# Turning a chunk's rows on VectorE and by small transfers in place of TensorE, in a block of a gated scan and a mixture of experts

## The chip, the cores and the metric

The kernel runs on one NeuronCore of a Trainium2 chip, in one launch. The metric is the device time in microseconds (us) of that core. The engines of a core work side by side, each through a queue of its own in program order: TensorE (PE, matrix products; its weight loads are PEld), VectorE (DVE), ScalarE (ACT), GpSimd (POOL) and SyncE (SP), which here only issues transfers. Engines wait for one another through semaphores. SBUF is the working memory of 128 partitions, PSUM the memory that TensorE writes to.

## The reference

`x` is [4, 1024, 256] in float32: 4 batches of 1024 tokens. The block is a modulated norm, a gated scan, a second modulated norm, and a mixture of 8 experts with the best two for each token:

```
mod = (silu(c) @ wmod).reshape(4, 6, 1, 256)      # sa, ca, ga, sb, cb, gb
h = layernorm(x) * (1 + ca) + sa

# the scan part
norm = sqrt(sum(h*h)) * D**-0.5
xn = rms_scale * h / (norm + 1e-8) * split_scale
K = sigmoid(xn @ W_K)                              # 256 -> 512
u, g_in, g_out = split(xn @ W_ugg, 3)              # 256 -> 3 x 512
u = u * sigmoid(g_in) * (1 - K)
s[t] = K[t-1] * s[t-1] + u[t]                      # along the tokens of a batch
x = x + ga * ((s * sigmoid(g_out)) @ W_out + h)

# the experts
h = layernorm(x) * (1 + cb) + sb
p = softmax(h @ Wg + bg); the best two, normed to 1
x = x + gb * sum over the two of p_e * (gelu(h @ W1[e] + b1[e]) @ W2[e] + b2[e])
```

## The kernel before

Tokens go through the first part in 8 chunks of 512 (two to a batch). A chunk lies in SBUF as [128 partitions, 4 groups, 256 channels]: token 128 n + p of the chunk is in partition p, group n. The products of the first part contract over channels, so the normed rows have to be turned: channels on partitions, tokens along the row, as `hT` [128, 2 halves of the channels, 512 tokens].

The order of the instructions on every engine is the order of the program text; nothing is reordered. One pass of the chunk loop (`c_`, from line 949) works on several chunks at once: the four quarters of the projections of chunk `c_` (`project`, quarters 0 to 3 of the 512 hidden channels), the preparation of the next chunk `nxt`, the output product and the second norm of the one before (`prv`), and the gate of the one before that (`old`). In a pass, TensorE does in order:

- `project(c_, 0)`: four products `pk`, `pgi`, `pu`, `pgo`, each of four matmuls with a moving operand of 128 x 512 taken from `hT`;
- `o_pe(prv)`: the output product `pya`, 32 matmuls;
- `f_turn(old)`: eight 128x128 turns of the second-norm rows `h2` into the PSUM tiles `ptf`, which ScalarE copies to `hT2` (L392);
- `project(c_, 1)`; then, in some passes, `r_rank_pe` (three small products, `pr`); then `f_gate(old)`: the router's 16 small products `pl`, with `hT2` as the stationary operand;
- `project(c_, 2)`; `project(c_, 3)`, in whose middle (between `pgi` and `pu`) stands `a_turn(nxt)`: eight turns of the scaled rows `u` of the next chunk into `pta`, which ScalarE scales by `rs_sb` and writes to `hT` (L390).

VectorE's work in a pass, around the change: in every quarter it takes `nu` (L431, which empties the PSUM tile of `pu`; L434), the scan (L440) and `z` (L441); ahead of quarter 2 `a_scale(nxt)` (L373 to L376) divides the rows `h` of the next chunk by their root mean square into `u`; ahead of quarter 3 `f_mod(prv)` (L484, L485) modulates the second-norm rows `h2`. The routing of a batch is spread over passes 3 to 7 and past the end: `r_softmax`, `r_first`, `r_second`, `r_place`; `r_second` ends with `chose`, `earlier` and `ended` (to L613), which `r_rank_pe` reads.

PSUM: `ps_mm` has four buffers, which `pk`, `pgi`, `pu`, `pgo` take in turn. The tile `u` has one buffer (tag "u"); `hT` has two, `hT2` one.

SP's queue issues every load and store of this part in program order: the load of `x` for chunk `c_ + 3` (L124), the store of `x` (`out_dram`, L467), the rows of the modulation (`mda`, `mdf`, `gb`, L312, L317, L325), `store_gb` (L329), the store of the second-norm rows `hx` (L495), and near the end the weights of the first blocks of experts (`fetch`, L804 to L807).

After the loop the work goes over into blocks of 256 tokens of one expert (`b_turn`, `b_up` with `ph`, `b_down` with `pye`), which gather rows of `hx` by lists that the routing wrote. The first two blocks are interleaved with what is left of the last chunk: `f_turn(last - 1)`, `r_second`, `b_up(0)`, `r_rank_pe`, `b_turn(1)`, `o_pe(last)`, `f_gate(last - 1)`, `f_mod_alone(last)`, `b_down(0)`, `f_turn(last)`, `b_up(1)`, `b_turn(2)`, `f_gate(last)`. The routing keeps a table `token` (L173) of the token number of each partition and group, which goes into the lists.

Chunk 0 is turned ahead of the loop, by TensorE, with code of its own (from L938).

Of the kernel before, what the change touches and what calls it, by code (L numbers as in the profile page):

```python
# [9 lines left out]
F32 = mybir.dt.float32  # L10
I32 = mybir.dt.int32
AF = mybir.ActivationFunctionType
# [7 lines left out]
def tile_adaln_block(  # L20
# [45 lines left out]
    TPB = TB // P  # L66
    TK = 256
    HK = TK // P
    LN_EPS = 1e-5
    RMS_EPS = 1e-8  # L70
    TOPK_EPS = 1e-8
# [92 lines left out]
    for e in range(E):  # L164
# [5 lines left out]
    nc.gpsimd.memset(again[:, :, 0:1], 0.0)  # L170
    count = const.tile([P, E], F32, tag="count", name="count")
    nc.gpsimd.memset(count, 0.0)
    token = const.tile([P, NT], F32, tag="token", name="token")  # L173
    nc.gpsimd.iota(
        token, [[P, NT]], base=0, channel_multiplier=1, allow_small_or_imprecise_dtypes=True
    )
    number = const.tile([P, NJ], F32, tag="number", name="number")
    nc.gpsimd.iota(
        number, [[1, NJ]], base=0, channel_multiplier=0, allow_small_or_imprecise_dtypes=True
# [191 lines left out]
    def a_scale(c_):  # L371
        h, ss, u = X[c_]["h"], X[c_]["ss"], X[c_]["u"]
        nc.vector.tensor_scalar_add(ss, ss, RMS_EPS)  # L373
        nc.vector.reciprocal(ss, ss)
        for n in range(TPB):
            nc.vector.tensor_scalar_mul(u[:, n, :], h[:, n, :], ss[:, n : n + 1])  # L376

    def a_skip(c_):

# [1 line left out]
        nc.vector.tensor_mul(h, h, wide_row(MDF[c_ // NB][:, 0, :]))  # L381
        nc.vector.tensor_add(xb, xb, h)

    def transposes(src, dst, what, scales):
        for k in range(KC):
            pt = ps_tr.tile([P, TB], F32, tag="tr", name=f"pt{what}_{k}")
            for t in range(TPB):
                nc.tensor.transpose(pt[:, ts(t, P)], src[:, t, ts(k, P)], ident)  # L388
            if scales:
                nc.scalar.activation(dst[:, k, :], pt, AF.Copy, scale=rs_sb[:, k : k + 1])  # L390
            else:
                nc.scalar.copy(dst[:, k, :], pt)  # L392

    def a_turn(c_):
        hT = deep.tile([P, KC, TB], F32, tag="hT", name=f"hT_{c_}")
        X[c_]["hT"] = hT
        transposes(X[c_]["u"], hT, f"a{c_}", True)

    def project(c_, hc, mid=()):


        hT = X[c_]["hT"]
        part = c_ % NB
        X[c_].setdefault("z", [])
        z = work.tile([P, TB], F32, tag="z", name=f"z_{c_}_{hc}", bufs=5)
        X[c_]["z"].append(z)
        kt = kts[part][hc]
        nu = work.tile([P, TB], F32, tag="nu", name=f"nu_{c_}_{hc}", bufs=2)
        go = work.tile([P, TB], F32, tag="go", name=f"go_{c_}_{hc}", bufs=2)

        def product(w, col, what):
            ps = ps_mm.tile([P, TB], F32, tag="mm", name=f"p{what}_{c_}_{hc}")
            for k in range(KC):
                nc.tensor.matmul(  # L414
                    ps,
                    lhsT=w[:, k, col : col + P],
                    rhs=hT[:, k, :],
                    start=(k == 0),
                    stop=(k == KC - 1),
                )  # L420
            return ps

        ps = product(wk_sb, hc * P, "k")
        nc.scalar.activation(kt[:, 1:], ps, AF.Sigmoid)
        if part < NB - 1:

            nc.scalar.activation(kts[part + 1][hc][:, 0:1], ps[:, TB - 1 :], AF.Sigmoid)
        nc.scalar.activation(nu, product(wu_sb, H + hc * P, "gi"), AF.Sigmoid)
        for step in mid:
            step()  # L430
        nc.vector.tensor_mul(nu, nu, product(wu_sb, hc * P, "u"))  # L431
        nc.scalar.activation(go, product(wu_sb, 2 * H + hc * P, "go"), AF.Sigmoid)

        nc.vector.scalar_tensor_tensor(nu, kt[:, 1:], 1.0, nu, ALU.subtract, ALU.mult)  # L434
        if part < NB - 1:
            s_ = ends[hc]
        else:
            s_ = work.tile([P, TB], F32, tag="s", name=f"s_{c_}_{hc}", bufs=2)
        first = 0.0 if part == 0 else ends[hc][:, TB - 1 :]
        nc.vector.tensor_tensor_scan(s_, kt[:, :TB], nu, first, ALU.mult, ALU.subtract)  # L440
        nc.vector.tensor_mul(z, s_, go)  # L441
# [56 lines left out]
            )  # L498
        )

    def f_turn(c_):
        hT = deep.tile([P, KC, TB], F32, tag="hT2", name=f"hT2_{c_}", bufs=1)
        X[c_]["hT2"] = hT
        transposes(X[c_]["h2"], hT, f"f{c_}", False)


    sh = [P, NT, E]
# [9 lines left out]
    def f_gate(c_):  # L517
        b, i = divmod(c_, NB)
        if i == 0:
            R[b] = {"p": small.tile(sh, F32, tag="p", name=f"p_{b}")}  # L520
        hT = X[c_]["hT2"]
        pl = ps_tr.tile([P, TPB, E], F32, tag="tr", name=f"pl_{c_}")
        for n in range(TPB):
            for k in range(KC):
                nc.tensor.matmul(  # L525
                    pl[:, n, :],
                    lhsT=hT[:, k, ts(n, P)],
                    rhs=wg_sb[:, k, :],
                    start=(k == 0),
                    stop=(k == KC - 1),  # L530
                )
        nc.vector.tensor_add(
            R[b]["p"][:, ts(i, TPB), :], pl, bg_sb.unsqueeze(1).broadcast_to((P, TPB, E))
        )
# [400 lines left out]
        all_rows(i)  # L935
    keep_busy(18)
    a_scale(0)
    hT = deep.tile([P, KC, TB], F32, tag="hT", name="hT_0")  # L938
    X[0]["hT"] = hT
    pts = [ps_tr.tile([P, TB], F32, tag="tr", name=f"pta0_{k}") for k in range(KC)]  # L940
    for t in range(TPB):
        for k in range(KC):
            nc.tensor.transpose(pts[k][:, ts(t, P)], X[0]["u"][:, t, ts(k, P)], ident)
    nc.scalar.activation(hT[:, 0, :], pts[0], AF.Copy, scale=rs_sb[:, 0:1])  # L944
    nc.vector.tensor_scalar_mul(hT[:, 1, :], pts[1], rs_sb[:, 1:2])
    other_rows()
    load_mdf(0)
    a_stats(1)
    for c_ in range(NCH):
        nxt, prv, old = c_ + 1, c_ - 1, c_ - 2  # L950
        more, was, been = nxt < NCH, prv >= 0, old >= 0
        b, part = divmod(c_, NB)

        route = old // NB if been and old % NB == NB - 1 else None
        placed = (c_ - 3) // NB if c_ >= 3 and (c_ - 3) % NB == NB - 1 else None


        if c_ + 3 < NCH:
            load_x(c_ + 3, nc.sync)
        if more:  # L960
            shift(nxt)
        project(c_, 0, [lambda: a_norm(nxt)] if more else [])
        drain(6)
        if more:
            a_mod(nxt)
        if was:
            a_skip(c_)
            o_pe(prv)
            o_resid(prv)
        if placed is not None:  # L970
            r_second(placed)
        if been:
            f_turn(old)
        if part == NB - 1:
            load_mdf(b + 1)


        if part == 0 and was:
            scale_out(b)
        if was:  # L980
            f_stats(prv)
        project(c_, 1, [lambda: a_square(nxt)] if more else [])
        if c_ == 0:
            first_contents()
        drain(6)
        if placed is not None:
            r_rank_pe(placed)
        if been:
            f_gate(old)
        if not more:  # L990
            fetch_weights(0)
            for j in range(NE):
                fetch_entries(j)

            wait_for(BK[0]["ld"], scattered)
            fetch_rows(0)
            fetch_rows(1)
        if part == 0:
            if c_ == 0:
                setup_ctx.close()  # L1000
                pools["w"] = ctx.enter_context(tc.tile_pool(name="weights", bufs=2))
            load_gb(b)
            load_mda(b + 1)
        elif c_ == 1:
            clear_rows()
            if c_ == 0:
                load_mdf(1)


        if more:  # L1010
            a_root(nxt)
        if was:
            shift(prv)
        if placed is not None:
            r_place(placed)
        if route is not None:
            r_softmax(route)
        if more:
            a_scale(nxt)
        project(  # L1020
            c_, 2,
            ([lambda: f_norm(prv)] if was else [])
            + ([lambda: r_exp(route)] if route is not None else []),
        )
        drain(6)
        if part == 0:
            store_gb(b)
        if c_ + 2 < NCH:
            a_stats(c_ + 2)


        if not was:
            a_skip(c_)
            scale_out(b)
        if was:
            f_mod(prv)
            f_store(prv)
        project(c_, 3, [lambda: a_turn(nxt) if more else b_turn(0)])
        drain(6)
        if route is not None:  # L1040
            r_first(route)
        if placed == EARLY_B - 1:
            tab["e"] = early_table()
# [1 line left out]

    last = NCH - 1
    fetch(0)
    f_turn(last - 1)
    r_second(B - 2)
    b_up(0)  # L1050
    r_rank_pe(B - 2)
# [6 lines left out]
    drain(4)  # L1058
    f_mod_alone(last)
    f_store(last)  # L1060
    b_down(0)
    f_turn(last)
    fetch(1)
    drain(6)
    b_up(1)
# [97 lines left out]
```

## Time and profile before

| | us |
|---|---|
| median of 3 runs (lowest, highest) | 818.54 (818.2, 821.06) |
| the profiled execution | 816.91 |
| its span, first to last instruction | 815.1 |
| first chunk's first product to last chunk's last product | 17.3 to 309.8 |
| eight turns `pta` or `ptf` on TensorE, from the first to the start of the next product | 0.87 |
| four matmuls of `pk` | 1.72 |
| ScalarE, two scalings of `hT` from `pta` | 1.26 |
| VectorE, four scalings of `u` | 1.14 |
| SP, one issue of a 512 KB store | 0.36 to 0.39 |
| landing of such a store, from its issue (median) | 3.3 to 3.7 |

The profiler records one execution: every instruction of every engine with its start and length. A row of the timeline merges neighbouring instructions of one line; matmul records overlap a little, since matmuls are pipelined, so the distance between the starts of two rows tells how long the first held TensorE. What ended a wait stands in brackets behind the idle time. The busy share of an engine is an average over stages that differ much.

### The profile page before, as it was taken

What the parts mean: (1) busy time and instruction counts of PE and PEld (TensorE: products, weight loads), DVE (VectorE), ACT (ScalarE), POOL (GpSimd) and SP (SyncE); (2) the same over time, 40 slices, a digit from 0 to 9 for tenths busy, and PEclk for the clock granted to TensorE, in tenths of its full rate; (3) what the DMA queues carried; (4) which work ended last, traced back from release to release, by engine and by line L of the source; (5) the groups of instructions that cost most, each with busy time, mean ns of one, the idle gap of its engine ahead of it and who ended that gap; (6) DMA issues with size and microseconds to landing.
All of it is one profiled execution on the core that took longest, in us unless ns stands there. A gap on an engine that the chain in (4) does not pass through costs nothing.

```text
span 815.1 us, 10691 instructions
## 1 busy us (share of the span) xinstructions
PE 800.9 (98%) x3479; PEld 608.3 (75%) x3479; DVE 350.1 (43%) x814; ACT 249.9 (31%) x574; POOL 299.1 (37%) x374
## 2 busy tenths in 40 slices
PE   8999999999999999999999999999999999999995
PEld 4464656464655558888888888888888888888984
DVE  5787776797688846554211211121121112112211
ACT  4434433535353243222222131222213122222231
POOL 2003010118203731788743433424343342434341
PEclk9999999999999999999999999999999999999998
DMA  8311231130102165598788687777777786776693
GB/s 286 118 42 56 86 101 49 52 98 26 46 26 85 27 181 170 146 255 200 197 238 242 177 237 202 218 197 221 203 210 232 204 226 196 212 196 191 195 292 81
DMA packets 107732, 130.76 MB, mean 160 GB/s; under 512 B 24647, under 2 KB 91787, under 8 KB 107665
## 3 DMA queue, kind: packets, MB, share of 16 engines
q1 hardware_dynamic: 88640, 104.11, 41.8%
q0 software_dynamic: 17456, 25.25, 13.9%
q10 hardware_dynamic: 1568, 0.57, 0.3%
q8 instruction: 34, 0.56, 0.3%
q14 instruction: 34, 0.27, 0.1%
HBM read 110.64 MB, written 21.75 MB: 162 GB/s over the span
## 4 chain that ended last, share of the span: by engine, by line
PE 94%; DMA 4%; DVE 1%; issue 0%; POOLq 0%; ACT 0%; SPq 0%; POOL 0%; DVEq 0%
PE ph_False L857 26%; PE pye_False L887 25%; PE pk L414 7%; PE pya L451 7%; PE pu L414 7%; PE pgo L414 7%; PE pgi L414 7%; DMA hb<-hx,ent 2%; PE ptx L841 2%; PE pl L525 2%; PE ptf L388 1%; PE pta L388 1%; DMA w<-in_L_ffn_W_dram 1%; PE idle L254 1%; PE pm L281 1%; DMA ent<-lists 1%
## 5 line engine op out<-in xcount | busy, mean ns | idle before, releaser
L887 PE MATMUL pye_False<-w,g_False 128*128 128x256 f32 x992 | 219.4, 379 | 0.0
L857 PE MATMUL ph_False<-xT,w 128*128 128x256 f32 x992 | 219.2, 379 | 0.0
L857 PEld LDWEIGHTS ph_False<-xT,w 128*128 128x128 f32 x992 | 188.3, 190 | 25.5
L887 PEld LDWEIGHTS pye_False<-w,g_False 128*128 128x128 f32 x992 | 186.1, 190 | 24.0
L866 ACT ACTIVATE g_False<-ph_False,bb 128x256 f32<-128x256 f32 x248 | 104.3, 473 | 312.8 <-issue 208.1
L874 POOL DMA_INDIRECT out_dram<-yb_False,ent x46 | 73.8, 1604 | 188.6 <-DVE yb_False L902 188.6
L843 DVE COPY xT<-ptx 128x512 f32<-128x512 f32 x37 | 25.6, 691 | 197.0 <-PE ptx L841 197.0
L901 DVE TENSOR_TENSOR yb_False<-pye_False,b2b 128x256 f32<-128x256 f32 x62 | 26.3, 425 | 154.7 <-PE pye_False L887 154.7
L544 POOL DMA_INDIRECT lists<-pay,placei x64 | 68.2, 1066 | 12.5 <-issue 11.5
L786 POOL DMA_INDIRECT hb<-hx,ent x56 | 59.0, 1054 | 18.7 <-issue 15.9
L414 PE MATMUL pk<-hT,wk_sb 128*128 128x512 f32 x128 | 60.9, 598 | 0.7 <-ACT hT L944 0.7
L414 PE MATMUL pu<-hT,wu_sb 128*128 128x512 f32 x128 | 60.2, 592 | 0.0
L414 PE MATMUL pgo<-hT,wu_sb 128*128 128x512 f32 x128 | 60.1, 592 | 0.0
L414 PE MATMUL pgi<-hT,wu_sb 128*128 128x512 f32 x128 | 60.1, 592 | 0.0
L214 POOL TENSOR_TENSOR rstd_f<-rstd_f,expo 128x4 f32<-128x4 f32 x8 | 8.2, 1019 | 132.5 <-DVE rstd_f L213 132.5
L451 PE MATMUL pya<-wo,z 128*128 128x256 f32 x256 | 56.6, 379 | 0.0
L451 PEld LDWEIGHTS pya<-wo,z 128*128 128x128 f32 x256 | 48.6, 190 | 9.5 <-issue 3.3
L414 PEld LDWEIGHTS pgi<-hT,wu_sb 128*128 128x128 f32 x128 | 24.3, 190 | 30.6 <-issue 30.4
L414 PEld LDWEIGHTS pgo<-hT,wu_sb 128*128 128x128 f32 x128 | 24.3, 190 | 30.6 <-issue 26.5
L414 PEld LDWEIGHTS pu<-hT,wu_sb 128*128 128x128 f32 x128 | 23.7, 190 | 26.8 <-issue 24.2
L414 PEld LDWEIGHTS pk<-hT,wk_sb 128*128 128x128 f32 x128 | 23.2, 190 | 24.5 <-issue 21.8
L431 DVE TENSOR_TENSOR nu<-nu,pu 128x512 f32<-128x512 f32 x32 | 22.0, 687 | 44.7 <-PE pu L414 33.0
(191 smaller groups left out, 760.9 us busy)
## 6 DMA issues: line engine op xcount, KB each, us to landing
w<-in_L_ffn_W_dram SPq DMA_DIRECT2D x72, 1024.0 KB, 6.5
b2b<-in_L_ffn_b_dram SPq DMA_DIRECT2D x36, 128.0 KB, 6.8
hx<-gb SPq DMA_DIRECT2D x4, 1024.0 KB, 4.8
out_dram<-x SPq DMA_DIRECT2D x8, 512.0 KB, 3.3
hx<-h SPq DMA_DIRECT2D x8, 512.0 KB, 3.7
x<-in_L_attn_x_dram SPq DMA_DIRECT2D x7, 512.0 KB, 5.3
wu_sb<-in_L_attn_W_ugg_dram SPq DMA_DIRECT2D x3, 512.0 KB, 5.5
mdf<-rows SPq DMA_DIRECT2D x4, 384.0 KB, 4.6
```

Of the source, the lines that this page charges most:

```text
L388: nc.tensor.transpose(pt[:, ts(t, P)], src[:, t, ts(k, P)], ident)
L414: nc.tensor.matmul(ps, lhsT=w[:, k, col : col + P], rhs=hT[:, k, :], start=(k == 0), stop=(k == KC - 1),)
L431: nc.vector.tensor_mul(nu, nu, product(wu_sb, hc * P, "u"))
L451: nc.tensor.matmul(py[:, t, :], lhsT=z[hc][:, ts(2 * q + t, P)], rhs=wo[:, hc, :], start=(hc == 0), stop=(hc == HC - 1),)
L544: ins = nc.gpsimd.indirect_dma_start(out=lists[:, :], out_offset=IndirectOffsetOnAxis(ap=place, axis=0), in_=what, in_offset=None, bounds_ ...
L786: nc.gpsimd.indirect_dma_start(out=g, out_offset=None, in_=hx[: seen(j), :], in_offset=IndirectOffsetOnAxis(ap=BK[j]["ent"][:, t, 0:1], ax ...
L843: nc.vector.tensor_copy(xT, pt)
L857: nc.tensor.matmul(ph[:, u, :], lhsT=w1[:, k, ts(fc, P)], rhs=xT[:, k, :n], start=(k == 0), stop=(k == KC - 1),)
L866: nc.scalar.activation(g[:, fc, :n], ph[:, u, :], AF.Gelu_apprx_tanh, bias=bb[:, fc : fc + 1])
L874: return nc.gpsimd.indirect_dma_start(out=out_rows[:n], out_offset=IndirectOffsetOnAxis(ap=at, axis=0), in_=yb, in_offset=None, bounds_che ...
L887: nc.tensor.matmul(py, lhsT=g[:, fc, ts(t, P)], rhs=w2[:, fc, :], start=(fc == 0), stop=(fc == FC - 1),)
L901: nc.vector.tensor_add(yb, py, b2b)
```

## The change

Only chunk 0 is still turned by TensorE. For chunks 1 to 7 `a_scale` writes the scaled rows in another order along the row (by quarter of the channels), `a_swap` then turns each 32 x 32 square in place with one VectorE instruction, and sixteen transfers on SP's queue, one for each pair of a source and a target quarter of the partitions, move 32 partitions x 1 KB each to their place in `hT`. `a_turn`, where it stood, only scales `hT` in place on ScalarE. `f_swap` does the same for the second-norm rows, with the reordering in the VectorE instruction, into a second tile of the tag "u" and by sixteen transfers into `hT2`; it stands after `f_store` ahead of quarter 3, one pass earlier than `f_turn` did for the same chunk. `hT` is now laid out [128, quarter of the source partitions, half of the channels, group, 32], so the moving operand of `project` is read in runs of 32 elements, and the router's logits come out with the tokens of a chunk in another order over partitions and groups, for which the table `token` is made anew by four instructions.

```diff
     token = const.tile([P, NT], F32, tag="token", name="token")
-    nc.gpsimd.iota(
-        token, [[P, NT]], base=0, channel_multiplier=1, allow_small_or_imprecise_dtypes=True
-    )
+    for n in range(TPB):
+        nc.gpsimd.iota(
+            token[ts(n, SQ), :].rearrange("p (c i) -> p c i", c=NB), [[TB, NB], [SQ, NQ]],
+            base=n * P, channel_multiplier=1, allow_small_or_imprecise_dtypes=True,
+        )
...
+        to = u.rearrange("p n d -> p (n d)").rearrange(
+            "p (q k n c) -> p n k q c", q=NQ, n=TPB, k=KC
+        )
         for n in range(TPB):
-            nc.vector.tensor_scalar_mul(u[:, n, :], h[:, n, :], ss[:, n : n + 1])
+            nc.vector.tensor_scalar_mul(
+                to[:, n], h[:, n, :].rearrange("p (k q c) -> p k q c", k=KC, q=NQ),
+                ss[:, n : n + 1],
+            )
...
-    def transposes(src, dst, what, scales):
+    turned = [P, NQ, KC, TPB, SQ]
+
+    def by_channel(hT):
+        return hT.rearrange("p i k n t -> p k n i t")
+
+    def swap(u, hT):
+        flat = u.rearrange("p n d -> p (n d)")
+        for q in range(NQ):
+            for i in range(NQ):
+                nc.sync.dma_start(
+                    out=hT[ts(q, SQ), i].rearrange("p k n t -> p (k n t)"),
+                    in_=flat[ts(i, SQ), ts(q, TPB * D // NQ)],
+                )
+
+    def a_swap(c_):
+        u = X[c_]["u"]
+        flat = u.rearrange("p n d -> p (n d)")
+        nc.vector.transpose(flat, flat)
+        X[c_]["hT"] = deep.tile(turned, F32, tag="hT", name=f"hT_{c_}")
+        swap(u, X[c_]["hT"])
+
+    def a_turn(c_):
+        hT = by_channel(X[c_]["hT"])
         for k in range(KC):
-            pt = ps_tr.tile([P, TB], F32, tag="tr", name=f"pt{what}_{k}")
-            for t in range(TPB):
-                nc.tensor.transpose(pt[:, ts(t, P)], src[:, t, ts(k, P)], ident)
-            if scales:
-                nc.scalar.activation(dst[:, k, :], pt, AF.Copy, scale=rs_sb[:, k : k + 1])
-            else:
-                nc.scalar.copy(dst[:, k, :], pt)
-
-    def a_turn(c_):
-        hT = deep.tile([P, KC, TB], F32, tag="hT", name=f"hT_{c_}")
-        X[c_]["hT"] = hT
-        transposes(X[c_]["u"], hT, f"a{c_}", True)
+            nc.scalar.activation(hT[:, k], hT[:, k], AF.Copy, scale=rs_sb[:, k : k + 1])
...
-                    rhs=hT[:, k, :],
+                    rhs=hT[:, k],
...
-    def f_turn(c_):
-        hT = deep.tile([P, KC, TB], F32, tag="hT2", name=f"hT2_{c_}", bufs=1)
-        X[c_]["hT2"] = hT
-        transposes(X[c_]["h2"], hT, f"f{c_}", False)
+    def f_swap(c_):
+        u = work.tile([P, TPB, D], F32, tag="u", name=f"u2_{c_}", bufs=1)
+        to = u.rearrange("p n d -> p (n d)").rearrange(
+            "p (q k n c) -> p n k q c", q=NQ, k=KC, n=TPB
+        )
+        nc.vector.transpose(to, X[c_]["h2"].rearrange("p n (k q c) -> p n k q c", k=KC, q=NQ))
+        X[c_]["hT2"] = deep.tile(turned, F32, tag="hT2", name=f"hT2_{c_}", bufs=1)
+        swap(u, X[c_]["hT2"])
...
-                    lhsT=hT[:, k, ts(n, P)],
+                    lhsT=hT[:, n, k],
...
-        if been:
-            f_turn(old)
...
         if more:
             a_scale(nxt)
+            a_swap(nxt)
         project(
             c_, 2,
...
         if was:
             f_mod(prv)
             f_store(prv)
+            f_swap(prv)
         project(c_, 3, [lambda: a_turn(nxt) if more else b_turn(0)])
...
     fetch(0)
-    f_turn(last - 1)
     r_second(B - 2)
...
     f_store(last)
+    f_swap(last)
     b_down(0)
-    f_turn(last)
     fetch(1)
```

More of the change, by code (lines that the diff above doesn't have):

```diff
@@ L68, in tile_adaln_block @@
     HK = TK // P
+    SQ = 32
+    NQ = P // SQ
     LN_EPS = 1e-5
@@ L374, in a_scale @@
         nc.vector.reciprocal(ss, ss)
+        if c_ == 0:
+            for n in range(TPB):
+                nc.vector.tensor_scalar_mul(u[:, n, :], h[:, n, :], ss[:, n : n + 1])
+            return
+        to = u.rearrange("p n d -> p (n d)").rearrange(
+            "p (q k n c) -> p n k q c", q=NQ, n=TPB, k=KC
+        )
         for n in range(TPB):
-            nc.vector.tensor_scalar_mul(u[:, n, :], h[:, n, :], ss[:, n : n + 1])
+            nc.vector.tensor_scalar_mul(
+                to[:, n], h[:, n, :].rearrange("p (k q c) -> p k q c", k=KC, q=NQ),
+                ss[:, n : n + 1],
+            )
     def a_skip(c_):
@@ L382, in a_skip @@
         nc.vector.tensor_add(xb, xb, h)
-    def transposes(src, dst, what, scales):
-        for k in range(KC):
-            pt = ps_tr.tile([P, TB], F32, tag="tr", name=f"pt{what}_{k}")
-            for t in range(TPB):
-                nc.tensor.transpose(pt[:, ts(t, P)], src[:, t, ts(k, P)], ident)
-            if scales:
-                nc.scalar.activation(dst[:, k, :], pt, AF.Copy, scale=rs_sb[:, k : k + 1])
-            else:
-                nc.scalar.copy(dst[:, k, :], pt)
-    def a_turn(c_):
-        hT = deep.tile([P, KC, TB], F32, tag="hT", name=f"hT_{c_}")
-        X[c_]["hT"] = hT
-        transposes(X[c_]["u"], hT, f"a{c_}", True)
+    turned = [P, NQ, KC, TPB, SQ]
[17 more added lines that the diff above has]
+        hT = by_channel(X[c_]["hT"])
+        for k in range(KC):
+            nc.scalar.activation(hT[:, k], hT[:, k], AF.Copy, scale=rs_sb[:, k : k + 1])
     def project(c_, hc, mid=()):
-        hT = X[c_]["hT"]
+        hT = by_channel(X[c_]["hT"])
         part = c_ % NB
@@ L520, in f_gate @@
             R[b] = {"p": small.tile(sh, F32, tag="p", name=f"p_{b}")}
-        hT = X[c_]["hT2"]
+        hT = X[c_]["hT2"].rearrange("p i k n t -> p i k (n t)")
         pl = ps_tr.tile([P, TPB, E], F32, tag="tr", name=f"pl_{c_}")
@@ L937, in tile_adaln_block @@
     a_scale(0)
-    hT = deep.tile([P, KC, TB], F32, tag="hT", name="hT_0")
-    X[0]["hT"] = hT
+    X[0]["hT"] = deep.tile(turned, F32, tag="hT", name="hT_0")
+    hT = by_channel(X[0]["hT"])
     pts = [ps_tr.tile([P, TB], F32, tag="tr", name=f"pta0_{k}") for k in range(KC)]
@@ L943, in tile_adaln_block @@
             nc.tensor.transpose(pts[k][:, ts(t, P)], X[0]["u"][:, t, ts(k, P)], ident)
-    nc.scalar.activation(hT[:, 0, :], pts[0], AF.Copy, scale=rs_sb[:, 0:1])
-    nc.vector.tensor_scalar_mul(hT[:, 1, :], pts[1], rs_sb[:, 1:2])
+    pts = [pt.rearrange("p (n i t) -> p n i t", n=TPB, i=NQ) for pt in pts]
+    nc.scalar.activation(hT[:, 0], pts[0], AF.Copy, scale=rs_sb[:, 0:1])
+    nc.vector.tensor_scalar_mul(hT[:, 1], pts[1], rs_sb[:, 1:2])
     other_rows()
```

## The prediction

> **What bounds the kernel now.** I read the busy shares first, then the chain of waits, then the timeline of each engine through the eight attention chunks (17 to 345 us).
>
> ```profile
> PE 800.9 (98%) x3479; PEld 608.3 (75%) x3479; DVE 350.1 (43%) x814; ACT 249.9 (31%) x574; POOL 299.1 (37%) x374
> ...
> PEclk9999999999999999999999999999999999999998
> ...
> PE 94%; DMA 4%; DVE 1%; issue 0%; POOLq 0%; ACT 0%; SPq 0%; POOL 0%; DVEq 0%
> ```
>
> TensorE (PE) is back to back and 94% of the chain that ends last is its work, so whatever leaves its queue is gained at once, unless something else is then late. VectorE's 43% hides this: by stretches of time it is busy 26.0 of 38 us from 119 to 157 us, but 35.85 of 39 us from 157 to 196 us (chunk 4) and 33.2 of 38 us from 234 to 272 us (chunk 6), where the routing is added. The end of chunk 4 in the timeline, TensorE first, then VectorE (columns: start, length, engine, line, operation, out and in, count):
>
> ```profile
> 189.77 1.88 PE L414 MATMUL pgi<-hT,wu_sb 128*128 128x512 f32 x4
> 191.49 1.04 PE L388 MATMUL pta<-ident,u 128*128 128x128 f32 x8
> 192.36 1.88 PE L414 MATMUL pu<-hT,wu_sb 128*128 128x512 f32 x4
> 194.08 1.88 PE L414 MATMUL pgo<-hT,wu_sb 128*128 128x512 f32 x4
> 195.80 1.88 PE L414 MATMUL pk<-hT,wk_sb 128*128 128x512 f32 x4
> ```
>
> ```profile
> 184.13 1.24 DVE L376 TENSOR_SCALAR u<-h,ss 128x256 f32<-128x256 f32 x4
> 186.61 0.69 DVE L431 TENSOR_TENSOR nu<-nu,pu 128x512 f32<-128x512 f32 x1 [1.23 <-PE pu L414]
> ...
> 193.04 1.23 DVE L485 TENSOR_TENSOR h<-h,mdf 128x1024 f32<-128x1024 f32 x1
> 194.35 0.69 DVE L431 TENSOR_TENSOR nu<-nu,pu 128x512 f32<-128x512 f32 x1
> ```
>
> Eight turns hold TensorE for 192.36 - 191.49 = 0.87 us. The chunk's input for the next (`u`) is ready at 185.37 and is wanted turned at 195.80: that window decides the case.
>
> **What goes.** `a_turn` loses 7 x 0.87 = 6.1 us of TensorE; `f_turn` 7 x 0.87 = 6.1 us in chunks 2 to 7 and just after them, and the last one 335.55 - 334.21 = 1.34 us. Sum **13.5 us**, all on the path. Two ScalarE copies a chunk from `ptf` (0.54 us each) go too; ScalarE is 31% busy, worth nothing.
>
> **What is added per swap.** (1) One VectorE turn of 128x1024. No row shows it; bounds are the four scalings (1.14 us per 1024) below and the scan (1.28 us per 512, so 2.56) above. It reads and writes each element once like L485, so I take 1.2. (2) Sixteen transfers of 32 KB on SP's queue. (3) Landing. (4) `a_turn`'s ScalarE scaling, now in place: 1.26 us for two today, 0.63 for the first, taken as the same.
>
> The timeline of SP's queue has its issues in pairs, and the list of transfers has the landing of a small one (KB each, median us from issue to landing, last):
>
> ```profile
> 157.27 0.36 SPq L495 DMA_DIRECT2D hx<-h  x1
> 157.68 0.50 SPq L124 DMA_DIRECT2D x<-in_L_attn_x_dram  x1
> 172.28 0.38 SPq L467 DMA_DIRECT2D out_dram<-x  x1
> 172.71 0.50 SPq L325 DMA_DIRECT2D gb<-rows  x1
> ```
>
> ```profile
> ent<-lists SPq DMA_DIRECT2D x28, 2.0 KB, 1.8
> ```
>
> SP needs 0.41 to 0.43 us from one transfer to the next, whatever its size. So the last of 16 starts 15 x 0.43 = 6.45 us after the first. Bounds: 0.31 (a 24 KB store of four rows, 0.27, plus 0.04) and 0.55. Landing: 1.8 to 1.9 us for `ent` (small) below, 4.1 us for `gb` (128 KB, one line read 128 times) above; a piece is 32 rows of 1 KB, nearest to `ent`: 1.9. With 0.07 from VectorE to SP, 0.63 for ScalarE and 0.15 of hand-overs a **swap takes 9.2 us** from the end of the turn to the first product it feeds (bounds 7.2 and 13.1).
>
> The Trainium skill (DMA: Bandwidth & Descriptors, "Anatomy of one DMA" and "Rules for kernel authors") speaks against this: a fixed cost of about 2.0 us for each transfer, and small ones under 64 KB are to be coalesced. Paid one after another that would be an estimated 16 x 2.08 = 33 us a swap and hundreds of us in all; SP's rows here show issues 0.4 us apart with 3 us landings overlapping, so I do not use it.
>
> **Windows against 9.2 us.** Each is from `u` ready plus 1.2 to the next chunk's first `pk`, less the 0.87 us that `pta` frees:
> - Chunk 0: 36.12 + 1.2 = 37.32 to 46.14 - 0.87 = 45.27, a window of 7.95: stall 9.2 - 7.95 = 1.25. Chunk 1: 72.89 to 80.52, 7.63: stall 1.57.
> - Chunks 2, 3, 5: 9.38, 9.32, 9.32: no stall, by a hair.
> - Chunk 4: VectorE has no idle time from 154.25 to 185.37, so the turn put in by `f_swap` at the end of chunk 3 (1.2 us, ahead of `nu`) arrives here whole, while TensorE comes 3 x 0.87 us earlier (the `pta` of chunks 3 and 4 and the `ptf` between): 185.37 + 2 x 1.2 = 187.77 to 195.80 - 2.61 = 193.19, 5.42: stall **3.78**. Chunk 6 likewise, 264.34 to 269.68: stall **3.86**. Here the wait takes the place of the turns removed.
> - Chunk 7: `f_swap(6)` stands ahead of `xT` and of the routing on VectorE. Today `ended` (L613) is done at 317.10 and `pr` (L631) starts at 317.55; with 1.2 more it is 318.30 against 316.68: 1.63 lost.
> - Last chunk: `h2` is done at 334.89, turned at 336.09, landed 8.5 later at 344.6 (no ScalarE). `pl` is wanted at 327.22 + 6.99 + 6.91 + 0.43 = 341.55: stall 3.0.
>
> Sum **15.1 us**. Net -13.5 + 15.1 = **+1.6 us**. On the profiled execution, 816.91 us (span 815.1 and 1.8 around it), that is 818.5; the median of the runs stands 1.63 higher, so **820.1 us**. 0.5% (4.1 us) is about what can be told from no change.
>
> **What I cost at nothing.** In chunks 0 to 3 and 5 VectorE's extra 1.2 to 2.4 us lie in its own waits for `pu` (2.2 to 3.3 us a chunk); without that cover it would be 1.2 us a turn, as in chunk 4. `nu` of quarter 3 slips to 159.1; its PSUM buffer is wanted at 159.8. Behind the swaps on SP stand the hidden-row store, `store_gb`, the `x` load (wanted some 30 us later) and, after chunk 7, two weight loads: `fetch(0)` slips from 309.3 to about 316.6, `fetch(1)` from 335.9 to 343, and with 6.5 us landing both are 4 us or more ahead of their `b_up`. `a_turn` now waits on ScalarE with `go` behind it, wanted by VectorE only later. `f_swap` shares `u` and waits for the reads of `a_swap`: landed at 155.8, needed 157.2, in chunk 3. Three more iotas (0.15 us) lie in GpSimd's 3.78 us of idling. Products read `hT` in runs of 32: two of 256 columns take 2 x 215.9 ns, one of 512 429.3, so a start costs 2.6 ns; I take no cost, the bound is 15 more starts x 2.6 ns x 512 products = 20 us.
>
> The three stalls of 3.0 to 3.9 us are the longest TensorE would have before the tail; the granted clock is 1.00 in every stage today, so no row prices them. The Trainium skill (TensorE: Matmul & The Clock Gate, "Part 1") puts a gate at an idle window of about 3.4 us, half speed until as long has been busy again: an estimate of 1.7 us each, 5 in all, on top of the sum.
>
> **Rivals.**
> - *Faster: short swaps.* Issues at 0.31 us make 7.2 us: stalls only in chunks 4 (1.78), 6 (1.86), last (1.0) and 7 (1.63), 6.3 in all, net -7.2: **811.3**. For: four-row store; against: no 128-partition issue was under 0.34. It decides from a swap under 8.0 us. Chance 0.25.
> - *Slower: pieces land late.* Landing 4.1 us as for `gb` makes 11.4 us: stalls 3.45 + 3.77 + 2.0 + 2.1 + 3.9 + 2.1 + 4.0 + 5.2 + 1.6 = 28.1 (what chunk 3 or 5 stalls, 4 or 6 saves), net +14.6: **833**. For: 16 pieces share 16 queues with scatters on GpSimd from 183 us. Against: 512 KB stores of 1 KB rows land in 3.3 us. Decides from 9.7 us. Chance 0.18.
> - *Slower: VectorE turns at the scan's rate*, 2.5 us: each window 1.3 shorter, 4 and 6 by 2.6, stalls 26.6, net +13: **831.6**. Or the products slow on 32-element runs: up to **840**. Chance 0.12 together.
> - *The change isn't what it says* (turns left on TensorE or the diff hiding them elsewhere): chunk 0 keeps its eight in any case; the others' code is gone. No weight.
>
> **How the numbers follow.** The forecast (a swap of 8.5 to 10.2 us, net -2.5 to +7.4) has 0.45, of it 0.28 within 0.5% and 0.17 above; its own range is 816 to 826. The first rival gives 0.22 faster and 0.03 same; the others are all slower. So faster 0.22, same 0.31, slower 0.47. Range 810 to 834: the first rival and most of the second; beyond are the bounds no row is near.
>
> **What would show it.** No `pta` or `ptf` but chunk 0's eight; VectorE turns of 1.2 us; 16 SP issues 0.43 us apart; TensorE waiting for ScalarE's `hT` before `pk`, most after chunks 4 and 6, and before the last `pl`. I am wrong if the swap is under 8 or over 10 us, if `pk` takes over 1.72 us for four products, or if TensorE waits for VectorE elsewhere.

## The result, and the profile after

The changed kernel takes 867.3 us (median of 4 runs, 865.93 to 871.55) against 819.8 us for the kernel before in the same comparison: a ratio of 1.0552, 95% interval 1.0494 to 1.0611. Ratios are of the fast runs alone, since the chip has a slower state for some executions, and so needn't be the quotient of two medians. It is 5.5% slower; the forecast was 820.1, the range 810 to 834. The profiled execution after is 865.93 us, its span 864.1 (before 815.1): 49.0 us to be accounted for.

From the page of the changed kernel, busy time of TensorE, its granted clock in 40 slices, and the chain of waits by engine:

```profile
PE 807.1 (93%) x3359; PEld 604.2 (70%) x3359; DVE 367.1 (42%) x829; ACT 241.0 (28%) x558; POOL 298.3 (35%) x377
...
PEclk9989999999899989989999999999999999999998
...
PE 76%; DVE 7%; DMA 5%; SPq 5%; ACT 3%; issue 2%; POOLq 0%; DVEq 0%; POOL 0%; ACTq 0%
```

TensorE has 120 matrix instructions fewer and yet 6.2 us more busy time. It is no longer 94% of the chain but 76%; SP's issues, 0% before, hold 5%; the clock row shows 8s among the attention chunks. TensorE's own list of waits (us in total, times, the longest) names where it stands still:

```profile
PE pk L443 <- ACT hT L426: 33.5, 7, 8.5
PE pl L558 <- DMA hT<-u: 6.8, 2, 6.2
```

Seven times, once a chunk, the first `pk` waits for the swapped rows. The end of chunk 2 in the timeline of TensorE (start, length, ..., in brackets the idle time before):

```profile
128.28 1.88 PE L443 MATMUL pgo<-hT,wu_sb 128*128 128x512 f32 x4
133.18 3.58 PE L443 MATMUL pk<-hT,wk_sb 128*128 128x512 f32 x4 [3.02 <-ACT hT L426]
136.55 2.02 PE L443 MATMUL pgi<-hT,wu_sb 128*128 128x512 f32 x4
138.41 1.88 PE L443 MATMUL pu<-hT,wu_sb 128*128 128x512 f32 x4
```

Two losses stand here one after the other: 3.02 us of idle time, and then four products in 3.58 us that take 1.88 elsewhere. From the start of `pk` to that of `pu` are 5.23 us in place of 3.44. The chain of waits through the same stretch says who was late:

```profile
129.82 0.59 SPq L411
130.41 0.04 issue
130.46 1.84 DMA hT<-u
...
132.40 0.73 ACT hT L426
```

SP starts its last issue at 130.46 us, the piece lands 1.84 us after that, ScalarE scales it from 132.40, and `pk` starts at 133.18. The timeline of SP's queue shows how long the issues took:

```profile
121.03 10.01 SPq L411 DMA_DIRECT2D hT<-u  x16
131.09 0.58 SPq L334 DMA_DIRECT2D hx<-gb  x1
```

Sixteen issues hold the queue for 10.01 us: one every 0.626 us, 0.59 for the issue and 0.04 between two. The forecast had 0.43. The table of stretches (us, busy time and count of PE, PEld, DVE, ACT and POOL, then the granted clock, the DMA share, GB/s) prices the second loss, just before and just after the stall:

```profile
128.00:130.00 2.00, 2.00 (x6) 0.61 (x4) 1.30 (x2) 0.00 (x0) 0.94 (x1) 1.00 0.21 56
...
133.00:136.50 3.50, 3.33 (x4) 1.32 (x5) 3.33 (x5) 1.22 (x3) 0.00 (x0) 0.56 1.02 343
```

The clock granted is 1.00 before the stall and 0.56 after it. So the account of the 49.0 us, by the prediction's own terms:

| Term | Forecast, us | Measured, us |
|---|---|---|
| turns gone from TensorE | -13.5 | -13.5 (the rows are gone; not timed by themselves) |
| waits of the first `pk` of chunks 1 to 7 | 10.5 | 33.5 |
| chunk 7, behind `f_swap(6)` on VectorE | 1.6 | 1.0 (0.6 for `xT`, 0.4 for `pr`) |
| last `pl` | 3.0 | 6.8 |
| lower clock after the stalls | not in the sum | 12.6 after the seven, 3.7 after the last |
| the rest | 0 | 4.9 (0.4 ahead of the first chunk, 2.8 in the block stage, 1.7 not traced) |

The 12.6 are the seven times from `pk` to `pu` less 3.44 (1.5 to 2.4 us each); the 3.7 are `pl` and `pye` at the end, 3.55 and 8.88 us in place of 1.71 and 6.99.

Chunks 4 and 6 stall longest (8.49 and 5.87 us). The chain shows a second thing in the last transfers of chunk 4:

```profile
209.18 6.42 DMA hT<-u
...
216.18 0.58 SPq L411
216.77 0.04 issue
216.81 4.25 DMA hT<-u
```

The last piece lands 4.25 us after its issue, not 1.84. An earlier one took 6.42, and by this chain the issue at 215.62 us had to wait for it, so the sixteen issues take 11.31 us in place of 10.01. In chunk 6 the last piece lands after 1.98 us; there one issue takes 1.73 us, and the sixteen 11.15.

### The profile page after: what moved, and what is told of

The parts are those of the page before. It is cut to its first block, busy times and chain, and to the rows that moved or that the text cites. A ratio compares the mean times of both kernels' runs of the same rounds, so it can differ in the third digit from the quotient of the medians.

```text
span 864.1 us, 10864 instructions
## 1 busy us (share of the span) xinstructions
PE 807.1 (93%) x3359; PEld 604.2 (70%) x3359; DVE 367.1 (42%) x829; ACT 241.0 (28%) x558; POOL 298.3 (35%) x377
## 4 chain that ended last, share of the span: by engine, by line
PE 76%; DVE 7%; DMA 5%; SPq 5%; ACT 3%; issue 2%; POOLq 0%; DVEq 0%; POOL 0%; ACTq 0%
PE pye_False L920 24%; PE ph_False L890 23%; PE pk L443 6%; SPq L411 5%; PE pya L480 5%; PE pgi L443 4%; PE pu L443 3%; DMA hT<-u 3%; PE pgo L443 3%; DMA hb<-hx,ent 2%; PE ptx L874 2%; PE pl L558 1%; PE ph_True L890 1%; PE idle L259 1%; PE pye_True L920 1%
## 5 line engine op out<-in xcount | busy, mean ns | idle before, releaser
L443 PE MATMUL pk<-hT,wk_sb 128*128 128x512 f32 x128 | 72.6, 697 | 34.2 <-ACT hT L426 33.5
L443 PEld LDWEIGHTS pk<-hT,wk_sb 128*128 128x128 f32 x128 | 26.2, 216 | 64.4 <-ACT hT L426 41.7
L577 POOL DMA_INDIRECT lists<-pay,placei x64 | 66.0, 1031 | 12.5 <-issue 11.5
L453 ACT ACTIVATE kt<-pk 128x512 f32<-128x512 f32 x32 | 19.2, 599 | 102.5 <-PE pk L443 97.3
```

Of the source, the lines that this page charges most:

```text
L443: nc.tensor.matmul(ps, lhsT=w[:, k, col : col + P], rhs=hT[:, k], start=(k == 0), stop=(k == KC - 1),)
L577: ins = nc.gpsimd.indirect_dma_start(out=lists[:, :], out_offset=IndirectOffsetOnAxis(ap=place, axis=0), in_=what, in_offset=None, bounds_ ...
```

## The experiments

Each says which part of the changed kernel is altered; the kernel before ran beside each.

**Which of the two swaps.** First, the scaled rows go back to TensorE and only the second-norm rows are swapped. The layout of `hT` stays that of the change, so the products still read runs of 32.

```diff
-        hT = by_channel(X[c_]["hT"])
         for k in range(KC):
-            nc.scalar.activation(hT[:, k], hT[:, k], AF.Copy, scale=rs_sb[:, k : k + 1])
+            pt = ps_tr.tile([P, TB], F32, tag="tr", name=f"pta{c_}_{k}")
+            for t in range(TPB):
+                nc.tensor.transpose(pt[:, ts(t, P)], X[c_]["u"][:, t, ts(k, P)], ident)
+            nc.scalar.activation(hT[:, k], pt.rearrange("p (n i t) -> p n i t", n=TPB, i=NQ),
+                AF.Copy, scale=rs_sb[:, k : k + 1])
...
-            a_swap(nxt)
```

> The scaled rows go back to TensorE (eight turns into pta, 0.87 us a chunk), the layout of hT in runs of 32 stays, the second-norm rows stay on VectorE and SP. Theory 1 (the swap of the scaled rows is too long: 16 issues at 0.625 us make 12.3 us from the end of the turn to the first pk, and each stall brings the clock down): all stalls before pk go; what stays is the last pl (6.3 us late, then some 4.3 us at a lower clock) and 2 us in chunk 7, against 7.4 us of turns saved: about 822 us on the profile. Rival (products on runs of 32 elements, or transfers in SBUF, slow TensorE itself): pk with four products stays over 1.72 us and the time over 840 us.

Measured: 822.27 us, as expected, ratio 0.9953 (0.9865 to 1.004). TensorE's waits have one entry of the swaps left, the last `pl`:

```profile
PE pl L555 <- DMA hT<-u: 5.3, 1, 5.3
```

Four products take 1.72 us again in every chunk, from the same runs of 32: the read order costs nothing. Most of the harm is in the scaled rows; the swap of the last chunk's second-norm rows costs these 5.3 us and 4.2 more, by which `pl` and `pye` behind the wait are slower. Second, the reverse: the scaled rows are swapped, the second-norm rows go back to TensorE (`f_swap` replaced by the former `f_turn` at its former places).

> The second-norm rows go back to TensorE, the scaled rows stay on VectorE and SP. Theory 1: the swap still takes 12.3 us against windows of 7.4 to 9.4 us, so stalls of 2.9 to 4.9 us before the first pk of chunks 1 to 7, 27.6 us in sum, and some 1.75 us of lower clock after each, 12.3 us, against 6.1 us of turns saved: about 851 us. Rival (the second swap does the harm, through the shared tile u and SP's queue, and the first is nearly hidden): about 820 us. No wait of VectorE for hT<-u in either case.

Measured: 863.88 us (859.4 and 868.37), ratio 1.0542 (1.0305 to 1.0779). The side was right, the size missed by 13 us, with an interval that is itself wide. Its waits:

```profile
PE pk L444 <- ACT hT L427: 34.5, 7, 7.5
```

34.5 us with no second-norm swap on VectorE or SP, 33.5 with it. So there is no sign that the 25.8 us for which VectorE waits in the changed kernel before it may overwrite the shared `u` (up to 7.7 us at a time) cost TensorE anything; but `f_turn` is back on TensorE here too, so the wait isn't tried by itself. The stalls of chunks 4 and 6, expected at 4.9 us at most, are 7.33 and 7.5, with landings of 6.12 and 4.27 us in chunk 4.

**What sets the pace of the issues.** Twice as many pieces of half the size:

```diff
-                nc.sync.dma_start(
-                    out=hT[ts(q, SQ), i].rearrange("p k n t -> p (k n t)"),
-                    in_=flat[ts(i, SQ), ts(q, TPB * D // NQ)],
-                )
+                for k in range(KC):
+                    nc.sync.dma_start(
+                        out=hT[ts(q, SQ), i, k].rearrange("p n t -> p (n t)"),
+                        in_=flat[ts(i, SQ), ts(q * KC + k, TPB * D // NQ // KC)],
+                    )
```

> Each swap in 32 pieces of 16 KB (32 rows of 512 bytes) in place of 16 of 32 KB. Theory (a queue spends 0.625 us on each issue or on each row of an issue once it issues without a pause, whatever the bytes): SP's issues of a swap take about 20 us, the stall before pk is 10 us longer in each chunk: 930 to 950 us. Rival (the pace is set by the bytes, 32 KB in 0.625 us): 32 issues some 0.31 us apart, 10 us in all as now, the time stays at 862 to 872.

Measured: 950.96 us (one run). All issues of the swaps, first in the changed kernel, then here (duration in ns: least, median, most; first and last start):

```profile
L411 SPq DMA_DIRECT2D hT<-u x240: 13/589/1883, 37.8 to 382.7; - x120
```

```profile
L412 SPq DMA_DIRECT2D hT<-u x480: 507/589/1916, 37.4 to 472.8; - x160
```

The same 589 ns for 16 KB as for 32 KB; a swap's issues now hold SP for 20.15 us and the seven waits of `pk` are 13.6 to 17.4 us. Bytes do not set the pace. The number of issues does, or the number of rows moved, which doubled with it; this run can't part the two (the version by DRAM, below, speaks against the rows).

Is the pace that of one queue, or shared? Half the pieces of the scaled rows are issued by ScalarE:

```diff
-        swap(u, X[c_]["hT"])
+        swap(u, X[c_]["hT"], [nc.sync, nc.scalar])
```

> The 16 transfers of the scaled rows are issued by SP and ScalarE in turn, 8 each; those of the second-norm rows stay on SP. Theory 1 in the form that the pace of 0.625 us belongs to the issuing queue: 8 issues take 5 us, the swap 7.3 us, the stalls in chunks 0 to 3 and 5 go, about 2 us each stay in chunks 4 and 6, and the end (the last pl) stays as it was: about 820 us. Rival (the pace is that of a shared generator or of the 16 DMA engines): the last issue is still 10 us after the first, about 866 us.

Measured: 879.0 us, ratio 1.0726 (1.0595 to 1.0858): both expectations missed. In chunk 0 each queue issues its eight at the same time, SP in 5.35 us, ScalarE in 5.06: the pace belongs to the queue that issues, and is not shared between the two. But ScalarE issues in its own instruction stream. Its timeline in chunk 0:

```profile
38.05 5.06 ACTq L411 DMA_DIRECT2D hT<-u  x8
43.16 0.60 ACT L453 ACTIVATE kt<-pk 128x512 f32<-128x512 f32 x1 [10.64 <-DMA hT<-u]
...
50.38 1.32 ACT L426 ACTIVATE hT<-hT,rs_sb 128x512 f32<-128x512 f32 x2
```

The last issue is out at 43.4 us, some 4.5 earlier than in the changed kernel, yet the scaling of `hT` starts at 50.38, later than the 49.43 there: `kt`, `nu` and `go` stood behind the issues, and TensorE waited for the PSUM they empty. A shorter swap was given back on the engine that carries it.

Fewer issues for the same bytes: the turned tile goes to DRAM in one transfer of 512 KB and comes back in four of 128 KB.

```diff
-        for q in range(NQ):
-            for i in range(NQ):
-                nc.sync.dma_start(...)
+        there = dram.tile([P, TPB * D], F32, tag="there", name=..., bufs=2)
+        nc.sync.dma_start(out=there, in_=flat)
+        by_q = there.rearrange("(i c) (q e) -> q c i e", i=NQ, q=NQ)
+        for q in range(NQ):
+            nc.sync.dma_start(out=hT[ts(q, SQ)].rearrange("p i k n t -> p i (k n t)"), in_=by_q[q])
```

> The turned tile goes to DRAM by one transfer of 512 KB and comes back by four of 128 KB, one for each quarter: five issues for sixteen, but two landings in a row. Theory (the count of issues sets the swap): 0.4 + 3.3 (landing of a 512 KB store of rows) + 4 x 0.6 + 1.9 to 4.1 + 0.63 = 8.6 to 10.8 us for 12.3 in an undisturbed chunk; stalls of 0 to 3 us in place of 3.2 to 8.7 and less of the low clock: 828 to 848 us. Rival (the bytes set the pace: 1 MB moved in place of 512 KB): the swap is 15 us or more and the time 890 or above.

Measured: 838.72 us, ratio 1.0238 (1.0209 to 1.0268), 28.6 us less than the changed kernel though each tile is moved twice. In chunk 2 the store is issued at 107.14 us; the timeline of all engines goes on:

```profile
109.81 1.74 SPq L415 DMA_DIRECT2D hT<-there  x4
...
114.23 1.33 ACT L429 ACTIVATE hT<-hT,rs_sb 128x512 f32<-128x512 f32 x2 [0.49 <-DMA hT<-there]
```

From the first issue to the first half scaled are 114.23 + 0.73 - 107.14 = 7.8 us, against 132.40 + 0.73 - 121.03 = 12.1 with sixteen pieces. Five of the seven first `pk` come with a wait of 0.22 us or none; what is left sits behind chunks 4 and 6 (9.9 us, and 7.0 for which the profile shows no releaser: longer than with sixteen pieces) and before the last `pl` (7.1).

The four loads also show what a single issue costs. All loads of this version together (duration in ns: least, median, most):

```profile
L415 SPq DMA_DIRECT2D hT<-there x60: 313/423/1097, 40.1 to 354.3; - x60
```

Such a load brings 128 KB in 128 rows of 1 KB, four times the rows of a piece, and yet takes 423 ns in place of 589, also as one of four in a row (1.74 us for the four). So rows don't set the pace by themselves: an issue from one part of SBUF to another takes longer than one that loads from DRAM. Why is open.

**What the clock costs.** TensorE turns the identity into a spare PSUM tile (24 to 74 times) ahead of the first `pk` of chunks 1 to 7, and 52 times ahead of the last `pl`, so that it isn't idle; the rows arrive no sooner.

```diff
+    def stay_warm(n, c_):
+        pt = ps_tr.tile([P, TB], F32, tag="tr", name=f"warm_{c_}")
+        for _ in range(n):
+            nc.tensor.transpose(pt[:, :P], ident, ident)
...
         project(c_, 3, [lambda: a_turn(nxt) if more else b_turn(0)])
+        if more:
+            stay_warm(WARM[c_], c_)
```

> Dummy turns of the identity are put on TensorE where it stands still (36, 41, 24, 29, 74, 26 and 50 ahead of the first pk of chunks 1 to 7, 52 ahead of the last pl; 0.11 us each, a little less than each stall): no other change. Theory 2 (the standstill lowers the granted clock, and the products after it run at half speed for up to 3.4 us): the first four pk take 1.72 us again in place of 3.2 to 3.6, the granted clock is over 0.99, and the time falls by 12.6 us in the chunks and some 4.3 us at the end, to about 850 us. Rival (pk is slow because of what it reads, fresh from the transfers): pk stays at 3.2 to 3.6 us and the time at 866 us or above.

Measured: 872.35 us, ratio 1.0645 (1.0585 to 1.0706), no faster than the changed kernel (1.0552). Ahead of chunks 1 to 4 and 6 it worked: `pk` takes 1.98 us, and the first `pya` of pass 4 comes at 175.75 us in place of 183.28. After chunk 4 it went otherwise:

```profile
205.71 6.93 PE L407 MATMUL warm<-ident 128*128 128x128 f32 x62
213.74 0.27 PE L407 MATMUL warm<-ident 128*128 128x128 f32 x1 [1.10 <-issue]
...
222.37 2.96 PE L449 MATMUL pk<-hT,wk_sb 128*128 128x512 f32 x4
```

The last dozen dummies come with gaps of up to 1.9 us for which the profile shows no wait (after chunk 6 the last four, up to 2.7 us). They end 6.0 us after the rows are there (6.8 after chunk 6), so they lengthen the stall, and the clock falls all the same. What makes the gaps wasn't found. The same again with the long fillings left out (nothing ahead of chunks 5 and 7 and of the last `pl`):

> Dummy turns of the identity fill TensorE's stall ahead of the first pk in chunks 1, 2, 3, 4 and 6 alone, where the fuller version had pk at 1.98 us again; nothing is added ahead of chunks 5 and 7 and of the last pl. Theory (half of the first two groups of products after a stall is lost to the clock): five times 1.5 to 1.9 us come back, 7.5 to 9.5 us: 857 to 860, ratio to the kernel before 1.046 to 1.050. Rival (the wait itself is what counts and the slow groups are made up for later): 864 to 869.

Measured: 856.89 us, ratio 1.0471 (1.0427 to 1.0516). The end of chunk 2:

```profile
125.80 2.78 PE L407 MATMUL warm<-ident 128*128 128x128 f32 x24
128.98 1.99 PE L449 MATMUL pk<-hT,wk_sb 128*128 128x512 f32 x4 [0.39 <-ACT hT L432]
```

The span falls by 8.2 us to 855.9, though no swap is shorter: in the five chunks with dummies, from the end of the turn to the first half of `hT` scaled are 12.2 to 12.8 us, as in the changed kernel. So the loss after a stall is real and is the clock's, and over all seven it is more than a third as long as the stalls themselves (12.6 to 33.5 us).

**Chunks 4 and 6.** GpSimd's scatters to `lists` run there. Twelve of them are moved from chunk 4's second half into chunk 5:

```diff
-        drain(6)
+        drain(12 if c_ == 5 else 6)
...
-        drain(6)
+        drain(0 if c_ == 4 else 6)
```

> GpSimd's twelve scatters to lists that lie beside the swap of scaled rows in chunk 4 (and at its end) go to the first half of chunk 5, ahead of chunk 5's swap. Theory (the scatters slow the issue and the landing of the pieces in chunk 4): the sixteen issues go back from 11.3 to 10.0 us and the last piece lands 1.9 us after its issue in place of 4.3 to 6.4: the stall before the first pk of chunk 5 falls from 8.65 to 4 to 5 us, the time by some 4 us to 862; chunk 6, untouched, keeps its 6.0. Rival (something else in chunk 4 delays them: VectorE's or SP's own work): the stall stays above 8 us and the time at 867.

Measured: 867.58 us, ratio 1.0591 (1.0562 to 1.0619), the stall after chunk 4 still 8.08 us, the numbers that the rival gave. But the edit didn't part the two as it was meant to. TensorE's stall doesn't hold GpSimd, which reached chunk 5's scatters at 213.26 us, before the swap was over. SP's sixteen issues, done by 216.05 and mostly ahead of them, took 10.02 us in place of 11.31; the last piece, beside them, took 5.27 us to land. So I left the first 32 scatters out altogether:

```diff
             place, what = waiting.pop(0)
+            left_out.append(place)
+            if len(left_out) <= 32:
+                continue
```

> The first 32 of GpSimd's scatters to lists (those that lie in chunks 4 to 7) are left out, so the places of the first half of the rows stay as they were preset; the rest is the changed kernel. Theory (the scatters slow the pieces): in chunk 4 and in chunk 6 the sixteen issues take 10.0 us and the last piece lands 1.8 to 2.0 us after its issue; the stalls of the next chunks' first pk fall from 8.65 and 6.0 us to 4 to 5 and 2.5 to 4, the time by 6 to 8 us to 858 to 861. Rival (the 1 MB store of gb that SP issues right behind the swap delays the last piece): landings of 4 to 5 us stay in chunks 4 and 6, time 864 to 868.

Measured: 859.69 us, ratio 1.0506 (1.0462 to 1.055), span 857.2. The swap of chunk 4 on SP, and the `pk` behind it on TensorE:

```profile
205.57 10.03 SPq L411 DMA_DIRECT2D hT<-u  x16
215.64 0.58 SPq L334 DMA_DIRECT2D hx<-gb  x1
```

```profile
217.74 3.78 PE L443 MATMUL pk<-hT,wk_sb 128*128 128x512 f32 x4 [4.70 <-ACT hT L426]
```

The stalls after chunks 4 and 6 fall from 8.49 and 5.87 us to 4.70 and 4.58, though the 1 MB store of `gb` still stands right behind the swap. From the end of the turn to the first half scaled are 12.26 and 12.16 us in place of 15.90 and 13.44, what the other chunks have: the scatters were the cause. Their price is 5.1 us of these two stalls; the waits for the last swap are 1.2 us shorter too, but nothing here shows that the scatters lengthened them. Of the 6.9 us by which the span falls, 1.7 lie in the block stage, whose lists lack half of their entries here, and 0.4 ahead of the first chunk; these don't come from the swaps.

**A version faster than both.** Swaps only where they have time. First with the sixteen pieces: second-norm rows of chunks 0 to 5 swapped, all else turned by TensorE.

> TensorE turns the scaled rows of every chunk and the second-norm rows of chunks 6 and 7; the second-norm rows of chunks 0 to 5 keep the swap. Theory (a swap costs nothing where its window is longer than some 12.3 us and TensorE's products don't mind runs of 32): six times 0.87 us of TensorE go and no stall comes, the last pl no longer waits: 818.5 - 5.2 = 813.3 us, ratio 0.993 to 0.995. Rival (the swaps that are left cost elsewhere: VectorE, the queue of SP, as the 0.56 us of xT and 5.28 us of pl in the version with all second-norm swaps hint): 818 to 822, ratio 1.0 or above.

Measured: 818.93 us (12 runs, 813.56 to 830.03) beside 819.6, ratio 0.9974 (0.9936 to 1.0011). No wait of a swap is left and the profiled span is 812.5, 2.6 us under that of before; but the interval holds no change, and the 0.6% expected isn't shown. Then by DRAM, wherever the full version by DRAM had no stall:

```diff
+    SWAPPED = (0, 1, 2, 3, 4, 5)
+    TURNED = (1, 2, 3, 4, 6)
...
-            a_swap(nxt)
+            if nxt in TURNED:
+                a_swap(nxt)
...
-            f_swap(prv)
+            if prv in SWAPPED:
+                f_swap(prv)
```

> By DRAM (one transfer out, four back) go the scaled rows of chunks 1, 2, 3, 4 and 6 and the second-norm rows of chunks 0 to 5, where the version with all swaps by DRAM showed no stall; TensorE turns the rest (scaled rows of 5 and 7, second-norm rows of 6 and 7). Theory (a move in some 10 us fits those windows and nothing else pays): 11 times 0.87 = 9.6 us of TensorE go: 808 to 811 us, ratio 0.986 to 0.990. Rival (VectorE's eleven turns in the full chunks 4 and 6, and the doubled traffic, cost elsewhere): 815 to 822, ratio 0.995 or above.

Measured: 811.06 us (6 runs, 807.48 to 812.63) beside 818.69, ratio 0.9909 (0.9878 to 0.994), span 808.2: 0.9% faster than the kernel before, a trifle short of the 1.0 to 1.4% expected. From the first `pk` to the last `pl` are 9.0 us less than before, close to the 9.6; the block stage behind them takes 2.0 us more, for a reason not found. TensorE's only wait for swapped rows:

```profile
PE pk L460 <- ACT hT L432: 0.2, 1, 0.2
```

## Why the prediction was wrong

**The step that failed** is "SP needs 0.41 to 0.43 us from one transfer to the next, whatever its size", and with it "a swap takes 9.2 us". Measured are 0.626 us, outside even the bounds given there (0.31 and 0.55): the last of sixteen issues starts 9.4 us after the first in place of 6.45. The swap takes 12.3 us in chunk 2 (turn done at 120.89, `pk` at 133.18).

The pace was wrong in two ways. It was read from pairs and stretched to sixteen, but the 0.41 to 0.43 us between two starts are only what the first issue holds; the second of the pairs shown takes 0.50 itself. Where SP's queue has three in a row before the change, most grow longer:

```profile
96.30 0.38 SPq L467 DMA_DIRECT2D out_dram<-x  x1
96.77 0.46 SPq L325 DMA_DIRECT2D gb<-rows  x1
97.27 0.94 SPq L312 DMA_DIRECT2D mda<-rows  x1
```

And it was taken to hold for every transfer. All the transfers that SP issues in the kernel before have DRAM on one side; none goes from SBUF to SBUF. The pieces do, and cost more from the first one on: 0.51 to 0.61 us for the first of a swap of scaled rows, mostly 0.59 for the others, while the four loads in a row of the version by DRAM stay near 0.43. The longest row of issues without a pause in the trace of before, four loads from 0.80 us on, goes at 0.45 to 0.50 us each and wouldn't have priced them either; what was missing is a row of their kind.

**The windows were right.** With 15 x 0.626 + 1.9 + 0.63 + 0.22 = 12.1 us in the forecast's own windows, the stalls are 4.2, 4.5, 2.7, 2.8, 3.9, 2.8 and 4.0 us (chunks 4 and 6 less the 2.8 that chunk 3 or 5 stalls). The version without scatters measured 4.39, 4.87, 3.02, 3.59, 4.70, 3.28 and 4.58. Because all windows lie between 5 and 9.4 us, near the forecast of the swap, 2.9 us more on a swap put a stall into the three chunks that were to have none and lengthened the other four. With 1.6 for chunk 7 and 5.8 for the last `pl` (measured 5.6 without scatters) the forecast's list would have come to 32.3 us in place of 15.1: 17.2 more.

**The clock was left out of the sum.** The forecast named it for the stalls of 3.0 to 3.9 us as an addition and priced the total without it. It cost 16.3 us in eight places, a third of the 49.0. The Trainium skill (TensorE: Matmul & The Clock Gate, "Part 1") has half the clock after an idle window of about 3.4 us, until as long has been busy again. The trace agrees on the loss (1.5 to 2.4 us each, for the 1.7 estimated from the page; up to 3.0 in other runs) and not on the threshold: the stall of 3.02 us in chunk 2 lost 1.8 us like the longer ones.

**Late pieces.** "Pieces land late" was a rival, with the scatters as its reason, at 2.2 us more for every swap. Among the scaled rows it was true in chunk 4 alone, with more there (landings of 4.25 and 6.42 us); in chunk 6 the scatters lengthened the issues. Without them 5.1 us of these stalls and 1.2 us of the waits for the last swap go, 6.3 in all.

The forecast had the profiled span grow by 1.6 us; it grew by 49.0. Of the 47.4 between them the pace is 17.2, the clock 16.3, what went with the scatters 6.3, the windows' misses of 0.2 to 0.8 us 3.5, and the rest of the table 4.9; 0.8 go off, since chunk 7 and the last `pl` without scatters cost that much less than listed.

**Right** were: what bounds the kernel; the 1.2 us for a turn on VectorE (1.25); 1.9 us for a landing (1.84); no cost for products on runs of 32; and chunk 7 and the last `pl` as places of loss. That the shared `u` would hurt nobody came out for another reason than the one given: by the forecast the rows would have landed 1.4 us before VectorE wanted the tile, measured are waits of up to 7.7 us while TensorE stands as well. The Trainium skill's rule against small transfers (DMA: Bandwidth & Descriptors, "Rules for kernel authors": under 64 KB, coalesce) was set aside since the 33 us a swap, sixteen fixed costs one after another, didn't fit the rows. The number didn't fit afterwards either (12.3 us), as the landings do overlap; the advice did: five transfers of 128 to 512 KB in place of sixteen of 32 KB took 28.6 us off the changed kernel.

## What to carry to other kernels

Price a burst of issues from a burst of the same kind of transfer. A pair shows only its first issue, and here transfers to and from DRAM didn't price pieces that stay in SBUF. If the trace has no such row, bound the pace widely: the pace of the queue times the count is a latency, and one queue's issues pass one by one. Where work leaves the engine that bounds the kernel for a path with latency, a window in which that path doesn't fit can be paid twice, in idle time and in the slower clock after it. Here every stall of 3.0 us and more was, so the second belongs into the sum together with the first. Move only where the window is wide: the same idea lost 5.5% everywhere and won 0.9% with fewer transfers in eleven places chosen from the profile.

## What the runs showed of the hardware

- A queue that issues small transfers from SBUF to SBUF one after another settles at 0.626 us an issue, for 32 KB and for 16 KB alike, where loads of 128 KB from DRAM go out every 0.43 us; SP and ScalarE side by side each keep a pace of that order (8 in 5.35 and 5.06 us). What in the queue sets it stays open.
- GpSimd's scatters, each of which moves next to nothing (16 of them and the rest of that queue 0.02 MB from 195 to 225 us), more than double the landing of pieces beside them, 1.84 to 4.25 us and more in chunk 4. How they do it stays open.
- Long runs of dummy turns on TensorE (74 and 50) came with unexplained gaps, up to 1.9 us in chunk 4 and 2.7 in chunk 6; runs of 24 to 41 had none.
